# A six-layer decoder on one core: new priority shifts for the kinds of steps in a hand-made schedule

## The chip, the cores and the metric

The kernel runs on one core of a Trainium2 chip. The metric is the device time of one execution in microseconds. Three runs of the kernel before gave 2013.14, 1996.82 and 2005.20 us; the median is 2005.2 us. The profile below is of a further execution that took 2008.77 us.

## What is computed

The input is `x` of 4 sequences, 512 tokens and 128 channels. Three sublayers follow, each with a residual and a layer norm after it:

```python
x = _layernorm(x + _L0_attn_ref(x, ...))            # decayed linear attention, 16 heads of 64
x = _layernorm(x + _L0_xattn_ref(ctx, ctx, x, ...)) # cross attention to 32 context tokens
x = _layernorm(x + _L0_ffn_ref(x, ...))             # six layers of local attention and FFN
```

The last sublayer takes most of the time. Its loop is:

```python
for i in range(6):
    x = attn_layer(shift_tokens(x), Wqkv[i], q_scale[i], k_scale[i], Wo[i]) + x
    x = ffn_layer(shift_tokens(x), ln_g[i], ln_b[i], W1[i], b1[i], W2[i], b2[i]) + x
```

In `attn_layer`, `q` and `k` are normalised per head and rotated, each block of 32 tokens attends to itself and to the block before it, and a projection follows. `ffn_layer` is a layer norm, a gated product with GELU, and a projection back.

## The kernel before

**Stages.** `Front` computes the first two sublayers, 32 pairs of heads (4 sequences, 8 pairs) by `pair`, and `cross` once a sequence. `Layers` computes the six layers. Its work is cut into 192 units: 6 layers, 4 sequences, 2 halves of the heads, 4 tiles of 128 tokens (line 1672). After the last tile of a sequence come `add_attention` and `ffn`. `load_half`, `load_values`, `load_tables` and `load_ffn` bring the weights of the next layer.

**What one unit does.** Line and engine of its steps, with the name under which the change speaks of them (a letter for the group, a number for the place in it):

| step | engine, line | work |
|---|---|---|
| u0, u5 | PE, 87 to 89 | projection of q, of k: three matmuls of 128x512 into one PSUM bank |
| u1, u6 | ACT, 1258 | square of that bank into `sq` (q, k) |
| u2, u3; u7, u8 | DVE, 1242 and 1251 | the two rotation products from the same bank (q; k) |
| u4, u9 | POOL, 1264 | sum of the two products (q, k) |
| u10 | DVE, 1275 | sums of squares |
| u11 to u14 | ACT and POOL, 1345 to 1352 | the factor `r`, one over the norm |
| q0, q2, q4, q6 | PE, 87 to 89 | in every other unit, four value projections, in a chain |
| q1, q3, q5, q7 | ACT, 1306 | their four evictions into `v` |
| q8 to q13 | SP, 1313 to 1325 | DMAs that regroup `v` by windows into `vb` |
| u15, u18 | POOL, 1362 | multiply by `r` (q, k) |
| u16, u19 | PE, 96 | four transposes (q, k) |
| u17, u20 | ACT, 1385 | evictions of these |
| u22 | PE, 1408 and 1421 | mask and 64x64 scores |
| u23, u24, u25; u26, u27; u28; u29 | DVE; ACT; DVE; POOL | softmax (lines 1441 to 1473) |
| u30, u31 | PE 1483, ACT 1487 | transposes of the probabilities, eviction |
| u32 | PE, 1499 | 64 products with `vb`, 32 rows each, into `O` |

In `Layers.ffn`, f0 to f6 normalise, f7, f9 and f11 are the gate products, f8, f10 and f12 add their bias, f13 is GELU, f14, f16 and f18 are the other three products, f20 is the last product (line 1625), f21 and f22 add to `X`. In `pair`, P0 to P39 are the steps of one pair of heads. The letters w, t, v, g and k are loads and splits of weights, I, C, W, O, D, V, S, N and X the rest of `Front`.

**What sets the order.** Nothing is reordered on the chip: each engine takes its instructions from its own queue in the order in which they are written. That order is made by `Plan.order`, a list scheduler which runs when the program is built. Every step has an engine, an estimated cost, what it depends on, and the buffers it holds (`Work.ROOM` says how many of each kind there are). When an engine comes free in the plan, it takes, among the steps that are ready and whose buffers are there, the one with the least priority number. In `Work.do` that number is the sum of a base (for a unit, its place i among the 192), a fixed offset, and `SHIFT` for the kind of step:

```python
name = f"{self.group}{self.count}"
self.plan.step(eng, cost, fn, r, w, prio=self.base + off + self.SHIFT.get(name, 0.0), **kw).name = name
```

A shift of +1 thus puts a kind of step behind its equals of one later unit. The plan gives a buffer back the moment the planned last step on it ends. On the chip the next user of a buffer waits on a semaphore. PSUM banks belong to the kinds `mm` (3), `tr` (2), `so` (2) and `f` (1); a projection takes one of the first three kinds and gives it back after its last reader.

Of the kernel before, what the change touches and what calls it, by code (L numbers as in the profile page):

```python
# [281 lines left out]
class Work:  # L282
# [5 lines left out]
        t1=8, t2=4, sq=2, nx=2, n2=3, r=4, u=2, v=2, qT=2, kT=3, pr=3, mx=3, su=3, pT=2, vb=2,  # L288
# [3 lines left out]
    )  # L292

    SHIFT = dict(
        C1=5.5, C2=8.5, C3=-2.75, D0=19.5, D2=12.75, D3=-11.25, D4=-0.5, D6=3.25, D7=12.25, D8=-1.25, D9=-7.75,
        D10=-7.25, I0=-0.5, I2=1.25, N0=1, N1=21.5, N2=0.5, N3=-14.75, N4=-22, N5=-27, N6=5.25, O0=-0.25,
        O1=-17.25, O2=-10.5, O4=-0.25, P0=-3.75, P1=14.25, P2=19.75, P3=-2.75, P4=13, P5=8.5, P8=-9.5, P9=-3.5,
        P10=-1, P11=125.75, P12=-12.5, P13=-2.25, P14=4, P15=4.5, P16=-4.5, P17=0.25, P18=42.75, P19=-0.25,
        P20=11.5, P21=40.5, P22=-0.75, P23=-26.75, P24=-1.25, P25=-0.25, P26=-3, P27=-0.75, P28=-7.5, P29=-0.75,
        P30=0.25, P31=18.5, P32=52.25, P33=-1.5, P34=3.75, P35=-24, P36=11.5, P37=-8.25, P38=7.75, P39=6, S0=-2,  # L300
        S1=18.25, S2=18, S3=24.75, S4=4.75, S5=3, S7=33.5, S8=-2, V0=-0.25, V1=48.5, V2=-82.5, V3=-19, V4=-27.25,
        V5=-11, V6=1.5, V7=19.25, W0=13.5, W1=-1.5, W2=-4, W3=21, W4=-4.5, W5=-2, W6=2, W7=-6.25, W8=-0.25,
        W9=-0.25, W10=4, W11=0.75, X1=28.25, X2=-0.5, X3=-1.75, X4=-2, X5=42.25, X6=3.25, X7=1.25, X8=127.5,
        X9=24.75, X10=-7.25, X11=0.25, X12=-0.5, X13=-6.75, X14=-4.75, X15=-11, X16=4.5, X17=-0.5, a0=-0.25,
        a1=-0.25, a2=4.25, a3=4.25, f0=-22.25, f1=-1.75, f2=54.25, f3=-5, f4=-30, f5=-5.5, f6=-5, f7=-9.25,
        f8=-26.25, f9=7.5, f10=1, f11=0.25, f12=-37.5, f13=-6.75, f14=-13.75, f15=-6.5, f16=0.5, f17=-46.5,
        f18=4.25, f19=-14.75, f20=8, f21=3.25, f22=-30.25, f23=8.5, f24=-6.5, f25=-39.75, f26=81.5, f27=5.25,
        f28=-61.75, f29=12.5, g0=-15.5, g1=1.25, g2=5.75, g3=0.75, g4=-1.5, g5=7.25, g6=-1.75, k0=-1.75, k2=-1.5,
        k3=12, k4=2, k5=-16, k6=17.5, k7=2, p0=33.5, p1=10.25, q0=2.25, q1=-2.25, q2=-10.25, q3=-4.75, q4=-0.25,
        q5=1.75, q6=0.75, q7=-16.25, q8=-23, q9=-9, q10=-2.75, q11=-6.75, q12=-1.25, q13=-22.5, t0=7.25,  # L310
        t1=-31.75, t2=-1, t3=-3.25, t4=-29, t5=-6.75, t6=6.75, u1=7.25, u2=2.25, u3=2.25, u4=-20.75, u6=-1.5,
        u7=2.25, u8=3.25, u9=-12.25, u10=-7.25, u11=40.25, u12=31.25, u13=-2, u14=-1.75, u15=-23.75, u16=9,
        u17=0.5, u18=-7.75, u19=1.25, u20=9.5, u21=34.75, u23=-12, u24=-59.75, u25=-14.5, u26=-23, u27=-53.5,
        u28=-45.5, u29=-49.75, u30=-29, u31=-36.25, u32=-58, v0=6.75, v1=-0.5, v2=2, v4=0.5, v5=5.25, v6=-2.75,
        w0=-19, w1=2, w2=-4, w3=-58.25, w4=35.5, w5=-17.75, w6=-3, w7=2.75, w8=3.25, w9=-1, w10=1.5, w11=-10,
        w12=-6, w13=-4.75, w14=2.5, w15=-1.75,
    )

    PE3, PE_T, PE_S, PE_AV = 0.73, 0.37, 0.72, 1.01
# [1501 lines left out]
```

## Time and profile before

| | us |
|---|---|
| three runs | 1996.82, 2005.20, 2013.14 |
| profiled execution | 2008.77 |
| its span, first to last instruction | 2007.1 |
| PE busy | 1850.5 |
| DVE busy | 1611.1 |
| ACT busy | 1587.4 |
| POOL busy | 1441.8 |

Queue q1, which carries the data transfers, took 45.7% of the time of 16 DMA engines. TensorE was granted 0.976 of its clock on average.

The costliest groups of single lines on each engine show that no line is dominant. On POOL the rotation sums (line 1264, both) take 500.0 us and the products with `r` (line 1362, both) 402.1 us. On DVE the sums of squares (line 1275) take 231.8 us, and the four rotation products 521.8 us. On ACT the `v` evictions take 219.8 us and the squares 231.7 us. On PE the products with `vb` take 210.9 us and the scores 169.8 us.

A group's line in the profile gives its busy time, the mean time of one instruction, and the idle time just before its instructions with the engine or transfer that ended it. Matmuls overlap each other, so their busy time is less than count times mean.

### The profile page before, as it was taken

What the parts mean: (1) busy time and instruction counts of PE and PEld (TensorE: products, weight loads), DVE (VectorE), ACT (ScalarE), POOL (GpSimd) and SP (SyncE); (2) the same over time, 40 slices, a digit from 0 to 9 for tenths busy, and PEclk for the clock granted to TensorE, in tenths of its full rate; (3) what the DMA queues carried; (4) which work ended last, traced back from release to release, by engine and by line L of the source; (5) the groups of instructions that cost most, each with busy time, mean ns of one, the idle gap of its engine ahead of it and who ended that gap; (6) DMA issues with size and microseconds to landing.
All of it is one profiled execution on the core that took longest, in us unless ns stands there. A gap on an engine that the chain in (4) does not pass through costs nothing.

```text
span 2007.1 us, 71083 instructions
## 1 busy us (share of the span) xinstructions
PE 1850.5 (92%) x28633; PEld 1405.3 (70%) x28633; DVE 1611.1 (80%) x3482; ACT 1587.4 (79%) x4048; POOL 1441.8 (72%) x1847
## 2 busy tenths in 40 slices
PE   7999999788898999989999999999999998999996
PEld 5676677566676777767777777777777776767675
DVE  5787786757787798886998868989788897888885
ACT  7877765689887788878888888888878897788785
POOL 3444444666777688886887878878878888787882
PEclk9999997789999999999999999999999999999999
DMA  3000001254555565665555555656655565545662
GB/s 90 1 6 2 1 2 34 67 130 109 133 148 123 131 152 139 156 150 147 133 132 146 146 146 142 166 123 160 150 142 144 125 157 149 142 107 134 146 172 60
DMA packets 146464, 233.02 MB, mean 116 GB/s; under 512 B 23770, under 2 KB 39000, under 8 KB 146136
## 3 DMA queue, kind: packets, MB, share of 16 engines
q1 hardware_dynamic: 146136, 228.46, 45.7%
q8 instruction: 228, 3.74, 0.8%
q14 instruction: 100, 0.82, 0.1%
HBM read 31.25 MB, written 2.10 MB: 17 GB/s over the span
## 4 chain that ended last, share of the span: by engine, by line
PE 57%; ACT 18%; DVE 14%; DMA 4%; issue 3%; SPq 3%; POOL 1%; DVEq 0%; ACTq 0%; POOLq 0%
PE O L1499 6%; PE s L1421 4%; PE pv L87 4%; DMA vb<-v 4%; PE pv L89 3%; PE pv L88 3%; PE ptk L96 3%; PE pp L1483 3%; PE ptq L96 2%; SPq L1325 2%; PE pyf L1625 2%; DVE nx L1275 2%; ACT sq L1258 2%; ACT v L1306 2%; PE pq L87 1%
## 5 line engine op out<-in xcount | busy, mean ns | idle before, releaser
L1264 POOL TENSOR_TENSOR t1q<-t1q,t2q 128x512 f32<-128x512 f32 x192 | 248.7, 1295 | 66.4 <-DVE t2q L1251 62.6
L1264 POOL TENSOR_TENSOR t1k<-t1k,t2k 128x512 f32<-128x512 f32 x192 | 251.3, 1310 | 55.4 <-DVE t2k L1251 40.7
L1473 POOL TENSOR_TENSOR pr<-pr,su 128x512 f32<-128x512 f32 x192 | 204.2, 1068 | 91.0 <-DVE su L1467 73.7
L1306 ACT COPY v<-pv 128x512 f32<-128x512 f32 x384 | 219.8, 602 | 42.7 <-PE pv L89 37.4
L1275 DVE TENSOR_REDUCE nx<-sq 128x16 f32<-128x1024 f32 x192 | 231.8, 1207 | 4.9 <-ACT sq L1258 3.7
L1499 PE MATMUL O<-vb,pT 128*32 128x128 f32 x6144 | 210.9, 279 | 10.5 <-DMA vb<-v 4.8
L1499 PEld LDWEIGHTS O<-vb,pT 128*32 128x32 f32 x6144 | 165.0, 111 | 63.3 <-issue 30.3
L1362 POOL TENSOR_TENSOR t1q<-t1q,r 128x512 f32<-128x512 f32 x192 | 201.2, 1051 | 2.7
L1362 POOL TENSOR_TENSOR t1k<-t1k,r 128x512 f32<-128x512 f32 x192 | 200.9, 1049 | 0.0
L1421 PE MATMUL s<-kT,qT 64*32 64x64 f32 x12288 | 169.8, 223 | 22.6 <-issue 22.5
L1460 ACT ACTIVATE pr<-s,mx 128x64 f32<-128x64 f32 x768 | 178.2, 325 | 9.8 <-DVE mx L1441 9.8
L1441 DVE TENSOR_REDUCE mx<-s 128x4 f32<-128x256 f32 x384 | 145.6, 413 | 42.7 <-PE s L1421 41.3
L1242 DVE TENSOR_TENSOR t1k<-pk,tl 128x512 f32<-128x512 f32 x192 | 130.7, 681 | 56.0 <-PE pk L89 34.8
L1242 DVE TENSOR_TENSOR t1q<-pq,tl 128x512 f32<-128x512 f32 x192 | 130.7, 681 | 50.7 <-PE pq L89 37.0
L1421 PEld LDWEIGHTS s<-kT,qT 64*32 64x32 f32 x12288 | 151.0, 105 | 25.0 <-issue 24.5
L1258 ACT ACTIVATE sq<-pk 128x512 f32<-128x512 f32 x192 | 116.1, 610 | 41.6 <-DVE t1k L1242 23.9
L1251 DVE TENSOR_TENSOR t2q<-pq,tl 128x512 f32<-128x512 f32 x192 | 130.0, 677 | 21.0 <-ACT sq L1258 20.1
L1466 DVE TENSOR_REDUCE su<-pr 128x8 f32<-128x512 f32 x192 | 129.3, 673 | 20.8 <-ACT pr L1463 12.0
L1251 DVE TENSOR_TENSOR t2k<-pk,tl 128x512 f32<-128x512 f32 x192 | 130.4, 679 | 18.8 <-ACT sq L1258 18.6
L1487 ACT COPY pT<-pp 128x512 f32<-128x512 f32 x192 | 113.3, 596 | 24.3 <-PE pp L1483 23.1
L1258 ACT ACTIVATE sq<-pq 128x512 f32<-128x512 f32 x192 | 115.6, 614 | 20.9 <-DVE t1q L1242 18.2
L96 PE MATMUL ptq<-ident,t1q 128*128 128x128 f32 x768 | 120.0, 280 | 11.6 <-DVE t2k L1251 4.6
(1002 smaller groups left out, 5428.3 us busy)
## 6 DMA issues: line engine op xcount, KB each, us to landing
vb<-v SPq DMA_DIRECT2D x576, 256.0 KB
vb<-v SPq DMA_DIRECT2D x192, 128.0 KB
vb<-v SPq DMA_DIRECT2D x288, 64.0 KB
vb<-in_c_zero_dram SPq DMA_DIRECT2D x96, 64.0 KB
wo<-in_L_ffn_Wo_dram SPq DMA_DIRECT2D x12, 256.0 KB
tb<-in_c_tabs_dram SPq DMA_DIRECT2D x12, 256.0 KB
w1r<-in_L_ffn_W_dram SPq DMA_DIRECT2D x6, 341.0 KB
xt<-in_x_dram SPq DMA_DIRECT2D x4, 256.0 KB
```

The costliest lines, as they stand in the source:

```text
L96: self.nc.tensor.transpose(bank[: blk.shape[1], tslice(t)], blk, self.ident)
L1242: nc.vector.tensor_tensor(out=t1(), in0=ps().rearrange("p (h d) -> p h d", d=DH), in1=tl()[:, 2 * j, t : t + 1, :].to_broadcast([P, 8, DH] ...
L1251: nc.vector.tensor_tensor(out=t2().rearrange("p h (z d) -> p h z d", z=2), in0=ps().rearrange("p (h z d) -> p h z d", d=32, z=2)[:, :, ::- ...
L1258: do("ACT", self.A512, lambda ps=ps, j=j: nc.scalar.activation(sq()[:, j], ps(), AF.Square), [ps], [sq])
L1264: lambda t1=t1, t2=t2: nc.gpsimd.tensor_tensor(out=t1(), in0=t1(), in1=t2(), op=ALU.add),
L1275: nc.vector.tensor_reduce(out=near()[:, :, 0], in_=sq().rearrange("p j (h d) -> p (j h) d", d=DH), op=ALU.add, axis=AX.X,)
L1306: do("ACT", self.A512, lambda pv=pv, j=j, e=e: nc.scalar.copy(v()[:, j, e], pv()), [pv], [v])
L1362: lambda x=x, j=j: nc.gpsimd.tensor_tensor(out=x(), in0=x(), in1=r()[:, j].unsqueeze(2).to_broadcast([P, 8, DH]), op=ALU.mult),
L1421: nc.tensor.matmul(sv[e]()[rows, p, :], lhsT=qT()[c, p, rows], rhs=kT()[c, p, 32 * w : 32 * w + 64], start=False, stop=True, skip_group_ch ...
L1460: nc.scalar.activation(pr()[:, a, 1], sv[1]()[:, a], AF.Exp, bias=mx()[:, a, 1:2])
L1473: lambda: nc.gpsimd.tensor_tensor(out=flat(), in0=flat(), in1=su().unsqueeze(2).to_broadcast([P, 8, 64]), op=ALU.mult),
L1499: nc.tensor.matmul(o[rows, t], lhsT=pT()[:, p, rows], rhs=vb()[:, t % 2, w, tslice(p)], start=(h2 == t == p == 0), stop=(h2 == 1 and p == ...
```

## The change

Only the numbers in `Work.SHIFT` change. No instruction, cost, buffer count or function does. Of the 249 kinds of steps 227 get a new number. These are the lines of the units, of the FFN, and of the pairs (a kind that is not listed has shift 0):

```diff
     SHIFT = dict(
...
-        D10=-7.25, I0=-0.5, I2=1.25, N0=1, N1=21.5, N2=0.5, N3=-14.75, N4=-22, N5=-27, N6=5.25, O0=-0.25,
-        O1=-17.25, O2=-10.5, O4=-0.25, P0=-3.75, P1=14.25, P2=19.75, P3=-2.75, P4=13, P5=8.5, P8=-9.5, P9=-3.5,
-        P10=-1, P11=125.75, P12=-12.5, P13=-2.25, P14=4, P15=4.5, P16=-4.5, P17=0.25, P18=42.75, P19=-0.25,
-        P20=11.5, P21=40.5, P22=-0.75, P23=-26.75, P24=-1.25, P25=-0.25, P26=-3, P27=-0.75, P28=-7.5, P29=-0.75,
-        P30=0.25, P31=18.5, P32=52.25, P33=-1.5, P34=3.75, P35=-24, P36=11.5, P37=-8.25, P38=7.75, P39=6, S0=-2,
...
-        a1=-0.25, a2=4.25, a3=4.25, f0=-22.25, f1=-1.75, f2=54.25, f3=-5, f4=-30, f5=-5.5, f6=-5, f7=-9.25,
-        f8=-26.25, f9=7.5, f10=1, f11=0.25, f12=-37.5, f13=-6.75, f14=-13.75, f15=-6.5, f16=0.5, f17=-46.5,
-        f18=4.25, f19=-14.75, f20=8, f21=3.25, f22=-30.25, f23=8.5, f24=-6.5, f25=-39.75, f26=81.5, f27=5.25,
-        f28=-61.75, f29=12.5, g0=-15.5, g1=1.25, g2=5.75, g3=0.75, g4=-1.5, g5=7.25, g6=-1.75, k0=-1.75, k2=-1.5,
-        k3=12, k4=2, k5=-16, k6=17.5, k7=2, p0=33.5, p1=10.25, q0=2.25, q1=-2.25, q2=-10.25, q3=-4.75, q4=-0.25,
-        q5=1.75, q6=0.75, q7=-16.25, q8=-23, q9=-9, q10=-2.75, q11=-6.75, q12=-1.25, q13=-22.5, t0=7.25,
-        t1=-31.75, t2=-1, t3=-3.25, t4=-29, t5=-6.75, t6=6.75, u1=7.25, u2=2.25, u3=2.25, u4=-20.75, u6=-1.5,
-        u7=2.25, u8=3.25, u9=-12.25, u10=-7.25, u11=40.25, u12=31.25, u13=-2, u14=-1.75, u15=-23.75, u16=9,
-        u17=0.5, u18=-7.75, u19=1.25, u20=9.5, u21=34.75, u23=-12, u24=-59.75, u25=-14.5, u26=-23, u27=-53.5,
-        u28=-45.5, u29=-49.75, u30=-29, u31=-36.25, u32=-58, v0=6.75, v1=-0.5, v2=2, v4=0.5, v5=5.25, v6=-2.75,
-        w0=-19, w1=2, w2=-4, w3=-58.25, w4=35.5, w5=-17.75, w6=-3, w7=2.75, w8=3.25, w9=-1, w10=1.5, w11=-10,
-        w12=-6, w13=-4.75, w14=2.5, w15=-1.75,
...
+        N6=25.75, O0=-2, O1=8.5, O2=-2.5, O3=2, O4=-1, O5=8.75, P0=-3.75, P1=11.5, P2=19.25, P3=-2.75, P4=5.25,
+        P5=18, P7=-15.75, P8=-0.75, P9=-3.5, P10=-4.75, P11=141, P12=0.25, P13=-2.25, P14=0.5, P15=-4, P16=-10.5,
+        P17=0.5, P18=57.5, P19=-0.5, P20=13.25, P21=26, P22=-0.75, P23=-51.5, P24=-1.25, P25=-0.25, P26=-2,
+        P27=-5.5, P28=-11.75, P29=-51, P31=25.75, P32=9.5, P33=-1.5, P34=3.5, P35=-12.5, P36=13.75, P37=-2.25,
...
+        X12=-3.5, X13=-4.5, X14=-5, X15=2.25, X16=6, a0=-3.25, a1=-8.75, a2=-2, a3=-1.5, f0=-9.75, f1=-1.5,
+        f2=52.75, f3=-0.5, f4=-69, f5=-2.5, f6=0.5, f7=4.5, f8=-38, f9=7, f10=-4.75, f11=-1.5, f12=-42.75,
+        f13=-8.75, f14=1, f15=-2.25, f17=-30.75, f18=3.5, f19=-5.5, f20=9.75, f21=1, f22=-56.75, f23=11.25,
+        f24=5.25, f25=-7.75, f26=44.75, f27=-3.5, f28=-50.25, f29=-6.75, g0=-25, g1=0.75, g2=5.5, g3=-3.5,
+        g4=5.25, g5=-4.75, g6=3.5, g7=11.5, k1=12.25, k2=-2, k3=9.5, k4=2, k5=7.5, k6=3, k7=14, p0=48.5, p1=11.5,
+        q0=2.25, q1=-1.5, q3=-20, q4=-0.5, q5=9.5, q6=0.25, q7=-7.75, q8=-15, q9=-3.75, q10=1, q11=4.75, q12=7,
+        q13=-5, t0=-6.75, t1=-52.5, t2=4.25, t3=-13.75, t4=-15.25, t5=1.25, t6=2.5, u1=8.75, u2=2, u3=2,
+        u4=-9.75, u6=4.5, u7=2, u8=2.5, u9=-20.25, u10=-7.5, u11=56.5, u12=30.75, u13=-2.5, u15=-22.75, u16=9.25,
+        u17=0.25, u18=-3.25, u19=1.25, u20=11, u21=34.5, u22=0.25, u23=-17.25, u24=-89.25, u25=-21.75,
+        u26=-22.75, u27=-74, u28=-45, u29=-24.25, u30=-14, u31=-50, u32=-42.75, v0=-1, v1=3, v2=-1.75, v4=-48.5,
+        v5=14, v6=-15.5, w0=-5, w1=-4, w2=-2.75, w3=-54.25, w4=56, w5=-5.75, w6=-5.75, w7=3, w8=3.25, w9=-5,
+        w10=1.5, w12=-1.75, w13=-3.5, w14=6.25, w15=1,
```

## What was predicted

> **What bounds the kernel now.** I read the busy table first, then the busy time by stretches, then who waited for whom, then the chain of waits and a piece of the timeline. The busy table gives engine, busy us, share and instructions:
>
> ```profile
> PE 1850.5 (92%) x28633; PEld 1405.3 (70%) x28633; DVE 1611.1 (80%) x3482; ACT 1587.4 (79%) x4048; POOL 1441.8 (72%) x1847
> ```
>
> PE leads, but no engine is far behind. In stretches (bounds, length, busy us of each engine with instruction counts, granted clock):
>
> ```profile
> 0.00:400.00 400.00, 363.94 (x2908) 266.64 (x2909) 296.87 (x774) 281.23 (x653) 186.34 (x223) 0.94 0.09 25
> 400.00:500.00 100.00, 84.14 (x1307) 64.53 (x1306) 66.84 (x146) 86.86 (x191) 67.17 (x89) 0.88 0.50 123
> 500.00:1950.00 1450.00, 1361.78 (x23758) 1043.63 (x23759) 1212.71 (x2468) 1186.03 (x3129) 1168.96 (x1510) 1.00 0.57 142
> 1950.00:2007.00 57.00, 40.69 (x679) 30.46 (x669) 34.69 (x97) 33.26 (x78) 19.30 (x27) 0.92 0.33 80
> ```
>
> PE idles 36.1 us in the first 400, 15.9 in the next 100, 88.2 in the 1450 of steady layers and 16.3 at the end: 156.5 us. An order can win no more than this, as long as PE's own work costs the same. The stretch from 500 on decides. By layer:
>
> ```profile
> 707.00:969.00 262.00, 247.08 (x4310) 189.31 (x4312) 220.16 (x446) 214.55 (x569) 212.59 (x276) 1.00 0.58 144
> 969.00:1229.00 260.00, 245.98 (x4304) 188.70 (x4296) 218.04 (x443) 213.91 (x568) 211.60 (x274) 1.00 0.58 143
> 1229.00:1487.00 258.00, 245.31 (x4312) 188.71 (x4308) 218.42 (x443) 214.10 (x568) 212.08 (x276) 1.00 0.58 147
> 1487.00:1744.00 257.00, 243.99 (x4284) 187.20 (x4278) 217.18 (x435) 212.88 (x566) 209.47 (x270) 1.00 0.58 144
> ```
>
> The bounds are those of the first `vb` products of each layer (I chose them so, to 1 us). The same work under the same shifts takes 257 to 262 us, since small differences carried from layer to layer change the order. That spread, 2%, is the measure of what a mere reshuffle does to one layer.
>
> Who waited for whom (waiting engine and line, releaser, us in total, times, longest) shows what is behind much of the idling:
>
> ```profile
> POOL pr L1473 <- DVE su L1467: 73.7, 48, 8.0
> POOL t1q L1264 <- DVE t2q L1251: 62.6, 64, 2.6
> ACT sq L1258 <- DVE t1k L1242: 23.9, 34, 2.6
> DVE t2q L1251 <- ACT sq L1258: 20.1, 29, 0.7
> DVE t2k L1251 <- ACT sq L1258: 18.6, 30, 0.9
> ACT sq L1258 <- DVE t1q L1242: 18.2, 26, 0.9
> DVE t1k L1242 <- ACT sq L1258: 16.3, 28, 2.0
> PE O L1499 <- DMA vb<-v: 4.8, 3, 2.1
> ```
>
> The square reads a projection's bank and the rotations read it too; neither uses a result of the other, and yet they wait for each other. The timeline shows it (start, duration, engine, instruction, idle time before with its releaser):
>
> ```profile
> 1013.29 0.65 DVE L1242 TENSOR_TENSOR t1k<-pk,tl 128x512 f32<-128x512 f32 x1
> ...
> 1014.61 0.69 DVE L1251 TENSOR_TENSOR t2k<-pk,tl 128x512 f32<-128x512 f32 x1 [0.66 <-ACT sq L1258]
> ```
>
> Between the two a square of `pk` ran; DVE stood still for 0.66 us. The plan counts the three readers as free to run together. It also gives a bank back at the planned end of the last one, so on the chip banks return late.
>
> **The change part by part.** No instruction comes or goes: added and removed work cost 0 us. Everything is moved, on all queues.
>
> *Units, PE.* u0, u5, q0 and u19 keep their shift, u16 and u22 gain 0.25. u32 and u30 stay ahead of all other unit steps (-58 and -29 become -42.75 and -14). q2 falls from -10.25 to 0, but it is chained behind q0, which comes at 2.25: when q0 was the least, q2 at 0 is nearly always the next least. f7 and f14 fall back by 14 and 15 units, f4 and a1 go ahead. A delay of 14 units of 8.1 us (260 us by 32 units) is 113 us, and the next layer's first unit on that sequence is 24 units, 195 us, behind: covered. I put PE's own moves at 0 us. If that cover failed, the price would be that of a missed FFN, its tail of about 24 us (the last products into `O` start at 1982.8, the span ends at 2007.1), per occurrence.
>
> *Units, the three readers.* On ACT the square of k goes from -1.5 to 4.5, behind the `q` evictions at 0.25; on DVE the rotations of q and k move together at 2, 2, 2 and 2.5. Pairing squares and rotations in order of time I count the square first in 132 of 192 units for k and 87 for q, last in 20 and 64, between the two rotations in 40 and 41. The new numbers favour the square last: DVE is no longer cut, ACT waits instead. Between 500 and 1950 waits between a square and a rotation total 94.1 us (DVE for a square 18.7, 17.7, 13.7 and 2.4; ACT for a rotation 23.4 and 18.2), of DVE's and ACT's idle 237.3 and 264.0 us: 19%. No row shows how much of that reaches PE. From below it is nothing (DVE and ACT are not the bound), from above all of PE's 88.2 us. I take the same 19%, 17 us, because PE's waits in this stretch are spread as widely as theirs. The converse is also possible, and is the second rival.
>
> This case's trace shows no square overlapping a rotation of its own bank in any of 384 pairs. The Trainium skill, "PSUM — Partial Sum Buffer", section "PSUM bank collisions raise a hardware error", says why: two engines must never access the same bank and quadrant at once, two readers included, and software has to keep them apart. By that rule an order can move this wait but not remove it: a bank is held for the sum of its readers whichever is first, and by it the term is 0 and not 17 us.
>
> *POOL.* u9 passes u4 (-12.25, -20.75 become -20.25, -9.75): k's sum first, as k's transposes already go first on PE (1.25 against 9.25). u29 stays first, since it belongs to a unit some places older. POOL idles 281 us from 500 on and its waits are for DVE; 0 us, and covered.
>
> *SP.* q8 to q13 all move back, by 4 to 17 units, past weight loads (w0, w3, w6, v4). Issues into `vb` take 576 x 0.735, 192 x 0.540, 192 x 0.645, 96 x 0.588 and 96 x 0.415 us by median, 747 us, 37% of the span: the queue has room. They stand in the chain of waits with 3.5% (70 us), but PE was idle for them 4.8 us, and its weight loads 2.7. Gain at most 7.5 us; loss bounded by the chain's 70. I take 0, near the wait row.
>
> *Pairs and transition.* PE's shifts in `pair` are unchanged to within 0.5 but for the group statistics; P29 and P32 (DVE and POOL, -0.75 to -51 and 52.25 to 9.5) go earlier. PE idles 10.9 us of the 250 from 50 to 300, so the gain there is 0 to 11; I take 2. From 340 to 500 it idles 29 us; ACT holds 32 table loads of 1.28 us at lines 1345 and 1346, two for each of the first 16 `r` steps. u11 (40 to 56.5) comes later, so a few of them fall behind the first GELU, which loads the right table once. Two units fewer give 5 us of ACT; I take 4, between 0 and 29. Start and end are 0.
>
> Sum: 2007.1 - 17 - 2 - 4 = 1984 us of span. The 1.7 us around the span and the 3.6 by which the profiled execution is over the median give 1982 us.
>
> **The rivals.** *A mere reshuffle.* The ranks of the busiest kinds hardly change, so the new order is another draw, four layers of which differ by 2%: their mean moves under 1%, 1995 to 2015, about 2003. For it: the PE shifts above. Against: 227 of 249 kinds move, those of DVE, ACT and POOL by several units.
>
> *Banks held longer, slower.* With the square last, a bank is given back by ACT's queue, after up to 0.66 us of waiting on DVE, where it was given back by DVE. If the 132 units where k's square came first each hold their bank for one square more (0.605 us), that is 80 us of bank time; with three `mm` banks, a third of it reaches PE, 27 us: 2032. It decides if PE's projections begin to wait for ACT's square. For it: ACT is 82% busy from 500 on. Against: PE waits now, 3.0 us for `ptk` and 4.6 for `ptq`, are for DVE's rotations, not for squares.
>
> *More than forecast.* If the order removes half of PE's idle time from 340 on (29 + 88.2 us, up to 1950), 58 us, it is 1947. For it: the same machine runs single 50 us stretches with 1.5 us of idle (1900 to 1950). Against: the 22.5 us inside scores with no releaser, which an order can't reach.
>
> **How the numbers follow.** Forecast 0.32 (1970 to 1992), more than forecast 0.13, reshuffle 0.30, slower 0.25. A change under 1% (20 us) can't be told here, since the three runs themselves span 16 us. Faster by over 1% is the forecast and the larger gain, less what of the forecast lies above 1985, 0.43; within 1% 0.32; slower 0.25. The range goes from 1947 to 2032, the ends of both outer cases.
>
> **What would show it.** If right: `sq` stands after both rotations for k in most units, waits of line 1251 for `sq` fall below 20 us in total (38.7 now), layers take 253 to 257 us, PE idles about 70 us from 500 to 1950. If PE's idle time before lines 87 and 96 with ACT's `sq` as releaser rises past 20 us, the slower rival holds. If the layers stay at 257 to 262 with other waits, it was a reshuffle. My sum falls if lateness of `vb` or of weights puts SP's queue in PE's waits.

## The result and the profile after

The kernel after takes 2020.43 us, the median of 12 runs (2013.23 to 2030.40). Beside it the kernel before took 2007.88, also of 12. The ratio of the two is put at 1.007 with an interval of 1.0049 to 1.009 (the medians alone give 1.006): slower by 0.7%. That is within 1% and inside the range, but on the other side of the forecast. The profiled execution of after took 2025.11 us with a span of 2023.4 and a mean granted clock of 0.971. Before had 2008.77, 2007.1 and 0.976.

The busy table of after:

```profile
PE 1853.1 (92%) x28633; PEld 1406.4 (70%) x28633; DVE 1615.5 (80%) x3482; ACT 1585.3 (78%) x4048; POOL 1439.7 (71%) x1847
```

All five are within 5 us of before, and the span is 16.3 us longer. By stretches: first four stages of the run, then the four middle layers (called 1 to 4 here, counting the six from 0), each from its first product into `O` to that of the next (bounds, length, busy us of PE, PEld, DVE, ACT, POOL with counts, granted clock, DMA share, GB/s):

```profile
0.00:400.00 400.00, 359.66 (x2894) 263.88 (x2895) 296.92 (x769) 278.83 (x649) 182.93 (x222) 0.94 0.08 23
400.00:500.00 100.00, 83.97 (x1316) 64.55 (x1315) 67.59 (x145) 87.21 (x190) 66.71 (x89) 0.90 0.54 127
500.00:1950.00 1450.00, 1355.15 (x23563) 1036.99 (x23565) 1205.57 (x2441) 1177.41 (x3111) 1160.48 (x1498) 0.99 0.60 141
1950.00:2023.00 73.00, 54.34 (x874) 40.99 (x865) 45.37 (x130) 41.89 (x100) 29.56 (x42) 0.91 0.38 92
708.00:977.00 269.00, 249.08 (x4284) 191.45 (x4276) 218.21 (x439) 213.25 (x567) 210.96 (x273) 0.97 0.59 138
977.00:1243.00 266.00, 248.14 (x4303) 190.27 (x4305) 219.43 (x448) 214.25 (x569) 212.37 (x274) 0.99 0.61 142
1243.00:1501.00 258.00, 244.01 (x4291) 187.11 (x4284) 218.16 (x439) 212.84 (x567) 210.96 (x274) 1.00 0.61 144
1501.00:1757.00 256.00, 244.56 (x4300) 187.08 (x4302) 218.71 (x440) 213.16 (x568) 210.38 (x273) 1.00 0.62 145
```

Two layers carry most of it. To a tenth of a us, the difference after less before is +2.0 up to the first `O` (422.9 to 424.9), then by layer -1.7, +8.5, +5.4, +0.9, -1.9, +1.1, and +2.0 in the tail: 16.3. Layers 1 and 2 are also those of the four in which the granted clock is below 1.00. Layers 3 and 4 are as fast as those of before.

Who waited for whom (waiting engine and line, releaser, us, times, longest; from the shift table on, line numbers are one less than before):

```profile
POOL pr L1472 <- DVE su L1466: 56.1, 52, 8.2
...
ACT sq L1257 <- DVE t1k L1241: 25.8, 34, 2.3
...
PE s L1420 <- issue: 24.1, 20, 3.2
...
ACT sq L1257 <- DVE t1q L1241: 21.0, 28, 1.4
DVE t1k L1241 <- ACT sq L1257: 20.1, 26, 2.3
...
DVE t2k L1250 <- ACT sq L1257: 18.3, 26, 1.1
DVE t2q L1250 <- ACT sq L1257: 15.0, 23, 0.7
DVE t1q L1241 <- ACT sq L1257: 14.0, 11, 5.2
```

The six waits between square and rotations total 114.2 us here and 109.5 before: the wait that the forecast wanted to shorten stayed. The other line to note is the third shown. PE's wait inside the scores has no releaser, and its longest rose from 2.3 to 3.2 us. The same line before, in the whole run, then that of layers 1 and 2 alone, after and before:

```profile
PE s L1421 <- issue: 22.5, 26, 2.3
PE s L1420 <- issue: 14.8, 10, 3.2
PE s L1421 <- issue: 9.3, 12, 1.5
```

The timeline of after shows one such wait (start, duration, engine, instruction; in brackets the idle time before):

```profile
903.40 0.70 PE L1420 MATMUL s<-kT,qT 64*32 64x64 f32 x46
903.75 2.13 SPq L1312 DMA_DIRECT2D vb<-in_c_zero_dram  x2
907.01 0.38 PE L1420 MATMUL s<-kT,qT 64*32 64x64 f32 x18 [2.91 <-issue]
907.32 1.12 PE L96 MATMUL f120pc<-ident,f120tn 128*128 128x128 f32 x4
908.09 0.78 PE L87 MATMUL pv<-wv11h,yh 128*128 128x512 f32 x1
```

PE stops for 2.91 us in the middle of 64 scores of one step, and the profile shows nothing that it waits for. The clock records show half clock from 907.3 on, for 3.4 us, and the projection matmul at 908.09 takes 0.78 us, where one at 899.94 took 0.40.

**Where these stalls lie.** I count all of PE's records from the first: matmuls, weight loads and the instructions that wait for semaphores. In both kernels the stalls of over 0.3 us inside a step of scores or of products into `O` then come after number 193 of every 256. The page's list of DMA queues has the one that brings the instructions:

```profile
q8 instruction: 227, 3.72, 0.8%
```

That is packets and MB (228 and 3.74 before): 16.4 KB a packet. PE has 58,314 records in after and 58,357 before, 257 and 256 to one packet. So PE's instructions arrive in blocks of 256, and PE stands still where a block ends and the next is not there. The transfers show it directly. Counted in order, a transfer starts 1.2 us (median) after PE passes a block end, 1.7 to 1.8 when the DMA engines are over 0.3 busy, and lasts 0.9 to 1.5. In the two kernels 60 block ends have a stall of over 0.6 us (from the start of one instruction to that of the next). In all 60 PE goes on 1.2 to 1.7 us after the landing of the transfer that belongs to the block end before. At the stall above, the transfer starts at 904.24 and lands at 905.51, and PE goes on at 907.01.

A long block hides these three times. A score step (144 instructions) followed by an `O` step (128) or another score step runs through a block in about 2 us and does not: 43 of the 60 stalls end a block that took PE under 3 us, and only 11 of the 394 other blocks were as short. What stalls is decided by which instructions the block ends fall on, and a new order deals these anew. The Trainium skill, "Advanced Engine Details and Errata", section "ISA Cache", gives a line of 16 KB, 256 instructions; the period counted here agrees.

From 500 us on, all eight stalls at block ends of 2.28 us or more in these two kernels (start to start) are followed or overlapped by half clock; the three of 2.04 to 2.12 are not. That is no threshold: in the traces of the twelve other kernels below, 38 stalls at block ends from 500 us on are as long, and 21 of them come with half clock, 17 without it, one of 3.50 us among these (at 1163.7 us, new order with 192 instructions ahead). Not all half clock comes with a block end, either. In layer 2 of after, the stretch at 1159.9 us follows a wait of 2.39 us ahead of an `O` step, after number 16 of 256 by the same count. PE goes on there, too, 1.38 us after a transfer of instructions has landed, but why it stops away from a block end is not explained.

The Trainium skill, "TensorE: Matmul & The Clock Gate", section "Part 1: The HAM clock gate (the "warmup" mystery)", asks for at least one idle window of about 3.4 us before the clock is halved. The half-clock stretches here are 3.4 us long, or twice that, but stalls of 2.28 to 3.18 us could be enough, and the measurement decides.

### The profile page after: what moved, and what is told of

The parts are those of the page before. It is cut to its first block, busy times and chain, and to the rows that moved or that the text cites. A ratio compares the mean times of both kernels' runs of the same rounds, so it can differ in the third digit from the quotient of the medians.

```text
span 2023.4 us, 71012 instructions
## 1 busy us (share of the span) xinstructions
PE 1853.1 (92%) x28633; PEld 1406.4 (70%) x28633; DVE 1615.5 (80%) x3482; ACT 1585.3 (78%) x4048; POOL 1439.7 (71%) x1847
## 4 chain that ended last, share of the span: by engine, by line
PE 56%; ACT 20%; DVE 15%; issue 4%; DMA 3%; SPq 2%; POOL 1%; ACTq 0%; DVEq 0%; POOLq 0%
PE O L1498 6%; PE s L1420 4%; PE pv L87 4%; DMA vb<-v 3%; PE pv L89 3%; PE pv L88 3%; PE ptk L96 3%; PE pp L1482 3%; ACT v L1305 2%; ACT sq L1257 2%; PE ptq L96 2%; DVE nx L1274 2%; ACT hidf L1585 2%; PE pyf L1624 2%; PE pk L87 2%
## 5 line engine op out<-in xcount | busy, mean ns | idle before, releaser
L1384 ACT COPY kT<-ptk 128x512 f32<-128x512 f32 x192 | 115.8, 603 | 22.3 <-PE ptk L96 22.0
## 6 DMA issues: line engine op xcount, KB each, us to landing
vb<-v SPq DMA_DIRECT2D x576, 256.0 KB, 5.0
wo<-in_L_ffn_Wo_dram SPq DMA_DIRECT2D x12, 256.0 KB, 4.4
tb<-in_c_tabs_dram SPq DMA_DIRECT2D x12, 256.0 KB, 3.8
xt<-in_x_dram SPq DMA_DIRECT2D x4, 256.0 KB
```

## Experiments

**One order at other places.** The theory: the slowdown is where block ends fall, and not the order's waits. Then a few instructions ahead of everything, which change nothing in the order, must move the time, and as many as a block must bring it back. The rival: the order itself waits more, and the time stays at 1.007. (PE's longest wait with a releaser, that of the mask for `qT`, did rise from 7.8 to 13.4 us.) The edit, for both orders, with 32, 64, 96 or 128 pairs of matmul and weight load (64 to 256 instructions):

```diff
         with tc.manual_schedule():
+            warm = k.tr("warm")
+            for _ in range(32):
+                k.nc.tensor.matmul(warm[:, 0:1], lhsT=k.identb, rhs=k.identb[:, 0:1], start=True, stop=True)
             for st in plan.order():
```

New order, 64 and 128 on:

> The changed kernel with 32 tiny matmuls (64 PE instructions, bf16, 1 column) ahead of everything; the order of all the rest is the same. Theory A (instruction fetch and clock): PE stands still where its stream runs out of fetched instructions, always at instruction 193 of a block of 256; stalls over 2 us are followed by 3.4 us at half clock, and in the profile of after six such half-clock windows (856 to 1177 us) cost layers 1 and 2 some 14 us. With the stream moved by 64 the block ends fall into other steps: the stalls of 2.9, 3.1, 2.3 and 3.3 us go from their places, the layers 1 and 2 take 258 to 264 us instead of 269.8 and 265.4, and the time falls by 5 to 14 us, to 2006 to 2015. Theory B (the order itself holds banks longer): order is the same, so the time stays at 2018 to 2023 and layers 1 and 2 stay over 265.

> The changed kernel with 64 tiny matmuls (128 PE instructions) ahead. Theory A: another draw of the same lottery, between 2005 and 2025, and it differs from the pad of 64 by over 4 us; the number of half-clock windows after 640 us goes with the time. Theory B: 2018 to 2023, within 2 us of the pad of 64.

Old order, 64 and 128 on:

> The kernel before with the same 32 tiny matmuls ahead. Theory A: its stalls move too; before was a lucky place (no half-clock window between 640 and 1820 us), so it can only stay or get worse: 2005 to 2022. Theory B: no change, ratio 0.999 to 1.001.

> The kernel before with 64 tiny matmuls (128 PE instructions) ahead. Theory A: 2003 to 2022, another draw. Theory B: ratio 0.999 to 1.001. If the mean of the padded versions of after is over that of before by 8 us or more, the order is worse whatever the place of the block ends; if the means agree within 4 us, the difference between the two kernels was that place.

Then 192 on for both, and a whole block for the new order:

> The changed kernel with 96 tiny matmuls (192 PE instructions) ahead, the last quarter of a block. Theory A: a fourth place of the block ends; a ratio between 0.997 and 1.009, and layers with a half-clock window over 264 us, those without one under 262. With the other three places it gives the mean of the new order over the places. If that mean is over the mean of the old order by 0.3% or more, the new order is itself worse; under 0.2%, the two orders are alike.

> The kernel before with 96 tiny matmuls (192 PE instructions) ahead. Theory A: between 0.998 and 1.006, with the same tie of slow layers to half-clock windows. Its mean over the four places is the measure for the old order.

> The changed kernel with 128 tiny matmuls ahead: 256 PE instructions, one whole block, so that the block ends fall into the same places of the same steps as in the changed kernel without a pad. Theory A (the place of the block ends decides): the time comes back to that of the changed kernel, 2015 to 2024, ratio 1.004 to 1.010, and layers 1 and 2 are the slow ones again (265 us or more), with half-clock windows near 856, 907, 958, 1160 and 1177 us. Theory C (any disturbance at the start leads to another course by chance): nothing ties it to the unpadded kernel; slow layers elsewhere or none, a ratio anywhere in 0.997 to 1.008.

Measured, as ratios to the kernel before, which ran beside each, with the intervals:

| instructions ahead | old order | new order |
|---|---|---|
| 0 | 1 | 1.0070 (1.0049 to 1.0090) |
| 64 | 0.9995 (0.9975 to 1.0016) | 0.9981 (0.9963 to 0.9999) |
| 128 | 1.0012 (0.9991 to 1.0033) | 1.0057 (1.0036 to 1.0078) |
| 192 | 1.0055 (1.0037 to 1.0073) | 1.0089 (1.0059 to 1.0119) |
| 256 | | 1.0092 (1.0062 to 1.0122) |

At 64 the new order is no longer slower: 2003.31 us against 2005.94, a little under the 2006 to 2015 that I expected. That is the lowest ratio of all these runs and the only one below 1 with its interval, if by 0.2%. The rival falls: PE's wait for `qT` is 13.4 us here too. The layers, in the same columns as above:

```profile
704.00:962.00 258.00, 244.04 (x4291) 187.36 (x4292) 218.29 (x440) 213.19 (x567) 211.51 (x274) 1.00 0.62 145
962.00:1221.00 259.00, 245.17 (x4306) 187.68 (x4308) 219.42 (x447) 213.97 (x569) 212.60 (x274) 1.00 0.62 146
1221.00:1478.00 257.00, 244.41 (x4304) 187.67 (x4296) 218.89 (x443) 213.56 (x568) 211.89 (x274) 1.00 0.62 146
1478.00:1735.00 257.00, 245.11 (x4304) 188.21 (x4296) 218.43 (x435) 213.47 (x567) 210.04 (x273) 0.99 0.62 144
```

The two long layers are gone, with the stalls and the half clock in them. PE's waits within these first two layers:

```profile
PE s L1419 <- issue: 7.0, 8, 1.6
```

At 256 the block ends are back on the same instructions, and so are the stalls. The same scores as in the timeline above:

```profile
900.03 0.70 PE L1419 MATMUL s<-kT,qT 64*32 64x64 f32 x46
903.64 0.38 PE L1419 MATMUL s<-kT,qT 64*32 64x64 f32 x18 [2.91 <-issue]
903.95 0.66 PE L96 MATMUL f120pc<-ident,f120tn 128*128 128x128 f32 x4
```

Again it stops after 46 scores of that step, for 2.91 us. Layer 1 takes 269.8 us as in after. Layer 2 takes 262.0, where after has 265.4 and I had put at least 265: one half-clock stretch there instead of two. That one comes again behind the wait ahead of an `O` step. The scores that stalled for 3.25 us at 1175.6 in after stall here, too, at 1169.0, but for 2.39 us and with no half clock behind. At 128 the long layers are the two others (256.7, 259.6, 265.9 and 268.0), and at 192 the time is spread (261.6 to 263.1, then 259.8). For the old order 64 and 128 decide little, since their intervals take in 1. The old order has its own bad places: layer 3 takes 267.8 us at 128, layer 2 takes 267.2 at 192.

Over the four middle layers of these nine kernels, 36 layers, a fit gives: time of a layer = 254.0 us + 0.85 x its stalls at block ends (those over 0.3 us) + 0.47 x its half-clock time. It explains 95% of the spread. Given these two, the new order's layer is 0.19 us shorter than the old one's, with a standard error of 0.35: no difference. Layers 1 and 2 of after have 20.9 us of stalls and 20.5 of half clock, before has 13.6 and 0. By the fit that is 0.85 x 7.3 + 0.47 x 20.5 = 15.8 us; measured were 13.9. A fit does not prove a cause; that the stalls leave with a shift of 64 and return with 256, and end at a fixed time after a transfer of instructions, does show that block ends place them. Which of them brings half clock is not shown.

**Heavy steps kept apart.** If the stalls come where heavy steps follow each other, an order that parts them should gain. In the planner's table of costs for one kind of PE step after another (S scores, O the products into `O`):

```diff
-("S", "O"): 0.27, ("O", "S"): 0.0,
+("S", "O"): 0.4, ("O", "S"): 0.3, ("S", "S"): 0.3, ("O", "O"): 0.3,
```

> The changed kernel with a plan that is told a price of 0.3 us for two score steps, two product steps, or a score and a product step in a row on PE (0.4 for a score step ahead of a product step, 0.27 before), so that the steps with 128 to 144 short instructions stand apart where other work is to be had. Theory A: the stalls inside these steps fall from 45.7 us to under 30, fewer than two half-clock windows lie between 640 and 1800 us (seven windows' time in the changed kernel), and the time falls to 1985 to 2008. If the stalls fall and the time doesn't, the order lost elsewhere what the stalls gave. If the stalls don't fall, what empties the stream isn't that these steps stand in a row.

Measured 1.0359 (1.0326 to 1.0392), 2074.57 us. The wait did shrink:

```profile
PE s L1420 <- issue: 11.1, 9, 2.8
```

Stalls inside steps (those over 0.6 us, start to start) fell from 45.7 to 15.1 us, yet half clock did not get less, and the layers take 286.3, 272.5, 265.5, 263.5, 272.3 and 256.0 us. The order lost far more than the stalls gave. Part of it is in PE's other waits; that for `vb` was 6.0 us in after:

```profile
PE O L1498 <- DMA vb<-v: 15.9, 8, 3.5
```

PE is also busy for 1875.5 us, where it was 1853.1. So the remedy failed because this order waits more elsewhere, and the run decides nothing on what the stalls cost.

**Fewer instructions in a score step.** The mask is put under the scores by eight 64x32 matmuls of a step; the edit uses one for all 128 rows of a half, and one more in the first tile. The same is computed (`idw` holds four copies of the 32-column identity side by side; besides, a row of ones is now taken from another tile, and its memset falls away):

```diff
-for w in range(4):
+for m in (1, 0) if t == 0 else (1,):
     for e in range(2):
         c = slice(e * 64, e * 64 + 64)
-        m = min(t + w, 1)
+        n = P if m else 32
         nc.tensor.matmul(
-            sv[e]()[32 * w : 32 * w + 32],
-            lhsT=k.identb[c, e * 64 : e * 64 + 32],
+            sv[e]()[:n],
+            lhsT=k.idw[c, :n],
             rhs=self.msk[c, m : m + 1, :].to_broadcast([64, 4, 64]),
-            start=True,
+            start=bool(m),
...
```

For the old order, and for the new one with 0, 64 and 128 instructions ahead:

> The same edit of the mask on the kernel before. Theory A: 1980 to 2003, ratio 0.988 to 0.999. Rival: 0.999 to 1.002.

> The changed kernel with the attention mask put into the score banks by two matmuls of 64 rows by 128 columns (four for the first tile of a sequence) in place of eight of 64 by 32: 2112 PE instructions fewer of some 58360, the planned order is the same. Theory A (each layer takes 254 us plus 0.85 of its block-end stalls plus 0.47 of its half-clock time, whatever the order): the sparser stream takes longer for a block, stalls at block ends fall below the changed kernel's 44 us, and the mask's own 0.35 us a unit falls by a half or less, 10 to 30 us: 1985 to 2010, ratio 0.990 to 1.002. Rival (PE's time isn't what the stalls and short instructions cost, the other engines hold the pace): ratio 1.003 to 1.010 as the changed kernel.

> The edit of the mask on the changed kernel with 32 tiny matmuls ahead (64 instructions): a second place of the block ends. Theory A: ratio 0.988 to 1.000; the layers lie on the same line of 254 us (less what the mask itself gives) plus stalls. If the two orders with this edit differ by less than the places do among themselves, the orders are alike.

> The same with 64 tiny matmuls ahead (128 instructions): a third place. Theory A: ratio 0.988 to 1.002, with the slow layers again those that have half-clock windows.

In this order they measured 1.0039 (1.0018 to 1.0060), 1.0042 (1.0019 to 1.0066), 1.0064 (1.0037 to 1.0091) and 1.0001 (0.9975 to 1.0026). Three of the four lie above the range that I expected, and the second lies in the rival's. The hoped-for gain did not come, though the stalls at block ends fell to 18.4, 15.0, 22.3 and 11.7 us (41.6 before, 44.3 after). The mask's line in the profile of before, then of the new order with this edit and no instructions ahead (count, then busy us, mean ns, idle before):

```profile
L1408 PE MATMUL s<-msk,identb 64*32 64x256 bf16 x1536 | 66.9, 279 | 11.5 <-ACT qT L1385 7.8 <-ACT sq L1258 1.4 <-DVE pr L1450 1.2
L1412 PE MATMUL s<-msk,idw 64*128 64x256 bf16 x384 | 58.9, 282 | 13.7 <-ACT qT L1389 13.2 <-ACT kT L1389 0.2 <-DVE pr L1454 0.2
```

Before, 1536 matmuls kept PE busy for 66.9 us; now 384 and 96 smaller ones (13.8) take 72.7. Each mean is about the same, 279 and 282 ns, so the narrow ones had overlapped. Over the 16 middle layers of these four kernels the same fit gives 256.7 us + 0.91 x stalls + 0.49 x half clock. The two prices are near those above; the base is 2.7 us a layer higher, and that took most of the gain back. Why the base rises was not tried further; the mask's 5.8 us more of PE are about 1 us a layer of it.

## Why the prediction was wrong

**The premise on the stalls.** The step that failed is in the argument against the largest gain: "the 22.5 us inside scores with no releaser, which an order can't reach". I took that idle time for a constant of the program. It is the part that the new order reached, by dealing the block ends anew: in layers 1 and 2 the stalls at block ends went from 13.6 to 20.9 us, and with them came 20.5 us of half clock, which no term of my sum had. Together that is 15.8 us by the fit, against 13.9 measured. That PE's own moves were put at 0 us is the same error: the cost of moving PE's steps lies in where the block ends fall, and by the table above it runs from 0.9981 to 1.0092 for one order. The forecast span was 1984 us and the measured one is 2023.4. Of the 39 us between them 16 are this slowdown, and 23 are the three gains, none of which came. PE idles 94.9 us from 500 to 1950, where I had put about 70 and before had 88.2.

**The three readers, -17 us: no gain seen.** The squares stayed where they were. For k the square is first in 128 of 192 units (132 before), between in 40 (40), last in 24 (20). For q it is first in 95 (87), between in 41 (41), last in 56 (64). My step from shift numbers to an order on the chip was wrong; a likely reason, not tested, is that a shift decides only among steps that are ready together. Line 1250 waits 33.3 us for `sq`, where I had put under 20 (38.7 before). The size had no row behind it either: in the whole run before, PE itself waited 1.7 us for squares and 11.4 for rotations, so even all of it is less than 17. The 19% was a share of other engines' idle time. No square overlaps a rotation of its own bank in after either, so the page by which this term is 0 had the better value, though the order was not moved far enough to test its rule.

**Pairs, -2 us, and transition, -4 us.** The last product into the pairs' `po` starts at 359.8 us instead of 356.9. The `r` steps still load 16 and 16 tables at lines 1344 and 1345, as before, and the table loads are 91 in all in both kernels. Both gains are absent. First `O` is 2.0 us late.

**The rivals.** The reshuffle was right in kind: equal layers once stalls and half clock are taken off, and a time under 1% away. But 2020 us lies above its 1995 to 2015, and it had no price for the block ends. Banks held longer is refuted as a mechanism: a bank is held 0.3 us longer after its last matmul (5.52 to 5.87 for q, 5.51 to 5.81 for k, medians), but PE does not wait for it. These are all of PE's waits for a square in after:

```profile
PE s L1407 <- ACT sq L1257: 1.4, 6, 0.2
PE pv L87 <- ACT sq L1257: 0.3, 1, 0.3
```

Before has the same two with the same times, and the rival needed over 20 us. That the kernel came out slower, as this rival said, has another reason. For POOL and SP the 0 us was about right: PE waits 6.0 us for `vb` (4.8 before), and its waits for POOL stay under 2 us in the layers.

**What stays open.** Over the four places the new order's mean ratio is 1.0052 (0 and 256 averaged) and the old one's 1.0016. The difference is 0.36%. Two marks were set ahead of the runs. By the first, the means at 64 and 128, the two orders are alike: 2.2 us apart, where under 4 was to count as alike. By the second, the mean over four places, the new order is itself worse from 0.3% on, and so it is, by some 7 us. The spread over places is 1.1% for the new order, three times the difference, so four places don't settle whether this order draws badly on the whole or only here. Part of the difference may be the start, where the first `O` comes at 424.2 against 422.0 on average; at 128 it was no later (421.0 against 421.4).

## What to carry to other kernels

Where an engine runs many short instructions, as PE does here, compare two orders at several places of the instruction blocks, for example with 64, 128 and 192 instructions put ahead, before a difference under 1% is put down to the order. Idle time without a releaser in the middle of a step, at a fixed count of instructions, is the sign of a late block, and it costs more when the clock is halved after it. Before one instruction replaces four, look whether the four overlap: here they did, and the one took PE longer.

## What the runs showed of the hardware

The time of one execution goes with its granted clock: over the 12 runs of after the correlation is -0.96, and 0.001 less clock comes with 1.8 us more (0.978 with 2014.2 us, 0.969 with 2030.4). By the fit, a half-clock stretch costs 0.47 of its length. How late the next block comes was not expected: its transfer starts 1.2 us after PE enters the block before it, and later beside busy DMA engines, lasts about 1 us, and PE goes on 1.2 to 1.7 us after it landed. In the 4 us up to the stall at 904 us the data transfers ran at 245 GB/s, with every DMA engine busy.
